# A pairwise bilinear kernel whose loads of fields and weights are asked for later in the text

## The chip, the cores and the metric

The kernel runs on one core of one Trainium2 chip. The metric is the device time of one execution in microseconds. Several executions are timed in rounds with executions of the kernel before on the same chip; ratios below are the mean time of one kernel's fast runs over that of the other's fast runs of the same rounds, so they are not quite the ratio of the medians.

## The reference

There are 32 fields of 128 numbers for 1024 rows, and for each of the 496 pairs i < j of fields a 128 x 128 weight. The output is 260 MB, so writing it is a large part of the work.

```python
I_IDX, J_IDX = pairs[:, 0], pairs[:, 1]          # all i < j of 32 fields, 496 pairs
v_i = inputs[:, I_IDX, :]                        # inputs: (1024, 32, 128) float32
v_j = inputs[:, J_IDX, :]
transformed = jnp.einsum('bpd,ped->bpe', v_i, W) # W: (496, 128, 128) float32
return transformed * v_j                         # (1024, 496, 128)
```

## The kernel before

The pairs are ordered by j, so that field j is first needed when j begins, after j(j-1)/2 pairs. Every field has a tile of its own and stays to the end. Weights come in chunks of eight pairs into four buffers. Two pairs share an output tile of 1 MB, and there are six such tiles.

```python
pairs = [(i, j) for j in range(1, 32) for i in range(j)]
xpool = tile_pool(name="x", bufs=1)      # tag=f"x{f}": a tile for each field
wpool = tile_pool(name="w", bufs=4)
opool = tile_pool(name="o", bufs=6)
ppool = tile_pool(name="ps", bufs=4, space=PSUM)
# ... load_x, load_w: dma_start of one field (512 KB) or one chunk (512 KB)
load_w(0, (0, 1, 3, WC))                 # on the ScalarE queue, three pieces
load_x(0, nc.sync, 2); load_x(1, nc.sync, 2); load_x(2, nc.sync)
load_w(1); load_x(3, nc.sync); load_w(2)
load_x(4, nc.scalar); load_x(5, nc.scalar)
for q, (i, j) in enumerate(pairs):
    if q % WC == 0 and q // WC + 3 < nchunk:
        load_w(q // WC + 3)              # three chunks ahead
    if i == 0 and 5 < j + 3 < NF:
        load_x(j + 3, nc.scalar)         # three fields ahead
    # two matmuls of 512 columns: po = w_q^T x_i
    # one VectorE product of 1024 columns: ot = po * x_j
    # after every second pair: dma_start of ot to the output, on the SyncE queue
```

Of the kernel before, what the change touches and what calls it, by code (L numbers as in the profile page):

```python
# [1 line left out]

# [4 lines left out]

F32 = mybir.dt.float32
ALU = mybir.AluOpType

P = 128
NF = 32
NQ = NF * (NF - 1) // 2
BT = 1024
HB = 512
WC = 8
OC = 2


def _pairs():  # L20

    return [(i, j) for j in range(1, NF) for i in range(j)]


@with_exitstack
def kernel(
    ctx: ExitStack,
    tc: tile.TileContext,
    xt: bass.AP,
    wt: bass.AP,  # L30
    out: bass.AP,
):






    nc = tc.nc
    pairs = _pairs()  # L40

    xpool = ctx.enter_context(tc.tile_pool(name="x", bufs=1))
    wpool = ctx.enter_context(tc.tile_pool(name="w", bufs=4))
    opool = ctx.enter_context(tc.tile_pool(name="o", bufs=6))
    ppool = ctx.enter_context(tc.tile_pool(name="ps", bufs=4, space=bass.MemoryType.PSUM))

    x_sb = {}

    def load_x(f, eng, pieces=1):
        x_sb[f] = xpool.tile([P, BT], F32, tag=f"x{f}", name=f"x_{f}")  # L50
        s = BT // pieces
        for k in range(pieces):
            eng.dma_start(out=x_sb[f][:, k * s : (k + 1) * s], in_=xt[:, f, k * s : (k + 1) * s])  # L53

    nchunk = NQ // WC
    w_sb = {}

    def load_w(c, splits=(0, WC)):
        w_sb[c] = wpool.tile([P, WC, P], F32, tag="w", name=f"w_{c}")
        for a, b in zip(splits, splits[1:]):  # L60
            nc.scalar.dma_start(out=w_sb[c][:, a:b, :], in_=wt[:, c * WC + a : c * WC + b, :])  # L61

    load_w(0, (0, 1, 3, WC))
    load_x(0, nc.sync, 2)
    load_x(1, nc.sync, 2)
    load_x(2, nc.sync)
    load_w(1)
    load_x(3, nc.sync)
    load_w(2)
    load_x(4, nc.scalar)  # L70
    load_x(5, nc.scalar)

    out_v = out.rearrange("q e b -> e q b")
    ot = None
    for q, (i, j) in enumerate(pairs):
        if q % WC == 0 and q // WC + 3 < nchunk:
            load_w(q // WC + 3)
        if i == 0 and 5 < j + 3 < NF:
            load_x(j + 3, nc.scalar)
        po = ppool.tile([P, BT], F32, tag="po", name=f"po_{q}")  # L80
        for h in range(0, BT, HB):
            nc.tensor.matmul(  # L82
                po[:, h : h + HB],
                w_sb[q // WC][:, q % WC, :],
                x_sb[i][:, h : h + HB],
                start=True,
                stop=True,
            )
        r = q % OC
        if r == 0:  # L90
            ot = opool.tile([P, OC, BT], F32, tag="ot", name=f"ot_{q}")
        if q < NQ - OC:
            nc.vector.tensor_tensor(ot[:, r, :], po[:, :], x_sb[j][:, :], ALU.mult)  # L93
            if r == OC - 1:
                nc.sync.dma_start(out=out_v[:, q - r : q + 1, :], in_=ot[:, :, :])  # L95
        else:
            for h in range(0, BT, HB):
                s = slice(h, h + HB)
                nc.vector.tensor_tensor(ot[:, r, s], po[:, s], x_sb[j][:, s], ALU.mult)  # L99
                nc.sync.dma_start(out=out_v[:, q, s], in_=ot[:, r, s])  # L100


# [25 lines left out]
```

## Time and profile before

| What | Before | How to read it |
|---|---|---|
| time, median of 3 | 877.84 us (877.59 to 878.51) | very steady, so 0.5% can be seen |
| span of the profiled run | 876.1 us | first to last instruction |
| PE busy | 856.6 us, 98% | TensorE is the bound over the whole |
| DVE busy | 606.3 us, 69% | the products lie beside the matmuls |
| DMA | 309.69 MB, mean 353 GB/s | 411 to 420 GB/s from 9 to 150 us, some 342 after |

In the views below PE stands for TensorE's matmuls, PEld for its weight loads, DVE for VectorE. A transfer is issued on the queue of an engine (ACTq for ScalarE, SPq for SyncE) and lands when the DMA engines have moved its bytes. A record is one entry of the trace; TensorE leaves four for each pair. The chain is the work that ended last, followed back to what released each step.

The means hide that there are two stages. After 150 us TensorE never stops. Before, the DMA engines are full, and TensorE is stopped at times.

### The profile page before, as it was taken

Reading aid. Unit: us, or ns where it says so; the run is one execution under the profiler, and the core shown is the slowest. Engines: PE = TensorE matmul, PEld = TensorE weight load, DVE = VectorE, ACT = ScalarE, POOL = GpSimd, SP = SyncE. Lnnn points to the kernel's source line nnn. Section 1 sums busy time; section 2 is a strip of 40 time slices with the busy share of each in tenths; the row PEclk is TensorE's granted clock in tenths of the full one; section 3 lists DMA queues with packets and bytes.
Section 4 is the critical chain, followed back from the end, with each engine's and each line's share of the span. In section 5 each row is a group of like instructions: output and inputs, shape, how many; then the busy total and the mean of one; then the engine's idle time right before and its main releaser. Section 6 shows DMA issues by size and latency. Waiting matters only on the chain.

```text
span 876.1 us, 5490 instructions
## 1 busy us (share of the span) xinstructions
PE 856.6 (98%) x1984; PEld 377.1 (43%) x1984; DVE 606.3 (69%) x498; POOL 0.2 (0%) x4
## 2 busy tenths in 40 slices
PE   8997899999999999999999999999999999999997
PEld 3432344444444444444444444444444444444443
DVE  4744677777777777777777777777777777777775
POOL 0000000000000000000000000000000000000000
PEclk9999999999999999999999999999999999999999
DMA  9999999989898898998988889888898989889877
GB/s 349 421 419 421 421 420 415 357 340 354 333 352 342 338 357 333 349 339 341 353 340 346 339 346 352 339 345 339 351 343 341 346 338 355 342 338 351 329 311 296
DMA packets 81898, 309.69 MB, mean 353 GB/s; under 512 B 5584, under 2 KB 5840, under 8 KB 81872
## 3 DMA queue, kind: packets, MB, share of 16 engines
q1 hardware_dynamic: 68624, 262.16, 75.3%
q10 hardware_dynamic: 13248, 47.19, 15.5%
q8 instruction: 15, 0.25, 0.1%
q14 instruction: 11, 0.09, 0.0%
HBM read 49.28 MB, written 260.05 MB: 353 GB/s over the span
## 4 chain that ended last, share of the span: by engine, by line
PE 88%; DMA 11%; DVE 0%; ACTq 0%; DVEq 0%; issue 0%; SPq 0%
PE po L82 88%; DMA x<-in_xt_dram 6%; DMA out_dram<-ot 3%; DMA w<-in_wt_dram 2%; DVE ot L93 0%; DVE ot L99 0%; DVEq L121 0%; ACTq L61 0%; ACTq L53 0%; DVEq L93 0%; SPq L95 0%
## 5 line engine op out<-in xcount | busy, mean ns | idle before, releaser
L82 PE MATMUL po<-x,w 128*128 128x512 f32 x1984 | 856.6, 594 | 13.9 <-DVE ot L93 9.9
L93 DVE TENSOR_TENSOR ot<-po,x 128x1024 f32<-128x1024 f32 x494 | 603.7, 1225 | 264.7 <-PE po L82 228.1
L82 PEld LDWEIGHTS po<-x,w 128*128 128x128 f32 x1984 | 377.1, 190 | 492.6 <-issue 470.0
L99 DVE TENSOR_TENSOR ot<-po,x 128x512 f32<-128x512 f32 x4 | 2.6, 687 | 0.9 <-PE po L82 0.9
L115 POOL MEMSET const-bfloat16-1.0<- 128x1 bf16 x1 | 0.1, 102 | 0.0
L115 POOL MEMSET const-uint8-127<- 128x1 uint8 x1 | 0.1, 102 | 0.0
L115 POOL MEMSET const-float32-0.0<- 128x1 f32 x1 | 0.1, 99 | 0.2 <-issue 0.2
L115 POOL MEMSET const-float32-1.0<- 128x1 f32 x1 | 0.1, 99 | 0.0
## 6 DMA issues: line engine op xcount, KB each, us to landing
out_dram<-ot SPq DMA_DIRECT2D x247, 1024.0 KB, 4.8
w<-in_wt_dram ACTq DMA_DIRECT2D x61, 512.0 KB, 4.3
x<-in_xt_dram ACTq DMA_DIRECT2D x28, 512.0 KB, 12.8
x<-in_xt_dram SPq DMA_DIRECT2D x4, 256.0 KB, 4.6
x<-in_xt_dram SPq DMA_DIRECT2D x2, 512.0 KB, 8.5
out_dram<-ot SPq DMA_DIRECT2D x4, 256.0 KB, 3.3
w<-in_wt_dram ACTq DMA_DIRECT2D x1, 320.0 KB, 6.3
w<-in_wt_dram ACTq DMA_DIRECT2D x1, 128.0 KB, 3.6
```

Source lines behind the costliest of these rows:

```text
L82: nc.tensor.matmul(po[:, h : h + HB], w_sb[q // WC][:, q % WC, :], x_sb[i][:, h : h + HB], start=True, stop=True,)
L93: nc.vector.tensor_tensor(ot[:, r, :], po[:, :], x_sb[j][:, :], ALU.mult)
L99: nc.vector.tensor_tensor(ot[:, r, s], po[:, s], x_sb[j][:, s], ALU.mult)
L115: nc = _bacc.Bacc("TRN2", target_bir_lowering=False, num_devices=1)
```

## The change

Its intent is to keep the early stage free of loads that are not yet needed: after a few early fields that keep a longer lead, a field is asked for one field ahead, and weights two chunks ahead instead of three. Nothing else differs.

```diff
     load_x(2, nc.sync)
-    load_w(1)
     load_x(3, nc.sync)
-    load_w(2)
-    load_x(4, nc.scalar)
-    load_x(5, nc.scalar)
+
+    def ahead(j):
+
+        return j + 3 if j <= 2 else j + 2 if j <= 5 else j + 1
...
     for q, (i, j) in enumerate(pairs):
-        if q % WC == 0 and q // WC + 3 < nchunk:
-            load_w(q // WC + 3)
-        if i == 0 and 5 < j + 3 < NF:
-            load_x(j + 3, nc.scalar)
+        if q % WC == 0 and q // WC + 2 < nchunk:
+            for c in (1, 2) if q == 0 else (q // WC + 2,):
+                load_w(c)
+        if i == 0:
+            for f in range(j + 1, min(ahead(j) + 1, NF)):
+                if f not in x_sb:
+                    load_x(f, nc.scalar)
```

## The prediction

> **What bounds the kernel now.** I read the page first, then the chain that ended last, the busy time in stretches, the waits of the SyncE queue, and the order of the issues on the ScalarE queue.
>
> ```profile
> span 876.1 us, 5490 instructions
> PE 856.6 (98%) x1984; PEld 377.1 (43%) x1984; DVE 606.3 (69%) x498; POOL 0.2 (0%) x4
> ...
> L82 PE MATMUL po<-x,w 128*128 128x512 f32 x1984 | 856.6, 594 | 13.9 <-DVE ot L93 9.9
> ...
> x<-in_xt_dram ACTq DMA_DIRECT2D x28, 512.0 KB, 12.8
> ```
>
> TensorE is the bound: there are 496 pairs, each with two matmuls of 512 columns, and the trace has 1984 records, so two per matmul and four per pair. The 594 ns are pipelined and overlap, so I take the pace from the chain instead:
>
> ```profile
> 42.11 14.41 DMA w<-in_wt_dram
> 56.54 12.74 DMA x<-in_xt_dram
> ...
> 69.31 15.24 DMA x<-in_xt_dram
> ...
> 97.73 772.78 PE po L82 x1800
> ```
>
> The last piece is 1800 records in 772.78 us, 0.4293 us each: 1.717 us per pair, and 1984 x 0.4293 = 851.7 us for the whole work. So only 876.1 - 851.7 = 24.4 us of the span are not matmuls at full pace. Before 97.7 us the chain is made of transfers, among them loads of weights and of fields: that is where the change can act. The same in stretches (columns: busy time of PE, PEld, DVE, POOL, then clock, DMA share, GB/s):
>
> ```profile
> 9.20:40.00 30.80, 30.80 (x73) 13.61 (x72) 22.49 (x19) 0.00 (x0) 1.00 1.02 411
> 40.00:97.70 57.70, 47.81 (x107) 19.29 (x105) 29.11 (x26) 0.00 (x0) 1.00 1.03 420
> 97.70:150.00 52.30, 52.27 (x122) 23.29 (x123) 39.04 (x33) 0.00 (x0) 1.00 1.02 418
> 150.00:870.50 720.50, 720.50 (x1679) 318.63 (x1677) 514.31 (x421) 0.00 (x0) 1.00 0.89 342
> ```
>
> From 9 to 150 us the DMA engines are full at 411 to 420 GB/s; afterwards 342 GB/s suffice and TensorE never stops. The loss is all in the second line: 107 records need 107 x 0.4293 = 45.9 us and the stretch has 57.7, so 11.8 us are lost. The remaining 12.6 us are the start (first matmul at 3.95 us, the first few at half pace, some 7 us together) and the tail of 5.6 us after 870.5; the change touches neither.
>
> Why are the DMA engines full early? The text of the kernel asks for field j+3 when field j begins, so field 31 is asked for at pair 28 x 27 / 2 = 378, which TensorE reaches at about 97.7 + (378 - 46) x 1.717 = 668 us. The trace has it otherwise. The issues on the ScalarE queue, in order (start, length of the run of issues, and how many):
>
> ```profile
> 0.73 3.35 ACTq L61 DMA_DIRECT2D w<-in_wt_dram  x5
> 4.64 3.63 ACTq L53 DMA_DIRECT2D x<-in_xt_dram  x2
> 10.06 0.34 ACTq L61 DMA_DIRECT2D w<-in_wt_dram  x1
> 10.44 12.57 ACTq L53 DMA_DIRECT2D x<-in_xt_dram  x5
> 23.11 0.43 ACTq L61 DMA_DIRECT2D w<-in_wt_dram  x1
> 23.57 18.44 ACTq L53 DMA_DIRECT2D x<-in_xt_dram  x8
> 42.11 0.44 ACTq L61 DMA_DIRECT2D w<-in_wt_dram  x1
> 46.68 16.10 ACTq L53 DMA_DIRECT2D x<-in_xt_dram  x8
> 64.22 0.33 ACTq L61 DMA_DIRECT2D w<-in_wt_dram  x1
> 67.22 12.52 ACTq L53 DMA_DIRECT2D x<-in_xt_dram  x5
> ```
>
> 2+5+8+8+5 = 28: all fields are issued by 79.7 us. They overtook the weight chunks that stand before them in the text. A fifth chunk has to wait for one of four buffers; a field has a tile of its own and waits for no buffer. So the build does not keep the order of the text on a queue: when the next load in the text has no buffer, it takes the next load that has one. And the outputs pay for it:
>
> ```profile
> SPq L95 <- DVE ot L93: 685.0, 234, 5.6
> SPq L95 <- DMA x<-in_xt_dram: 67.8, 17, 7.2
> ```
>
> The issue of an output waited 17 times, 67.8 us in all, for the landing of a field. The compiled program of the kernel before (the change was not built) says why: all transfers of both queues use eight completion semaphores in turn, and each waits until the transfer eight places earlier has landed.
>
> **What the Trainium skill says.** All from the page "DMA: Bandwidth & Descriptors". Section "Issuing engines are not separate DMA queues": transfers issued by different engines end up on the same 16 DMA engines and interleave. The trace agrees: loads on one queue and outputs on the other together make the 420 GB/s. Section "Specifications" gives a fabric ceiling of 435 GB/s and about 358 per core at the memory; the trace's plateau of 420 is near the first and above the second, so with this mix the second is not the limit. Section "Anatomy of one DMA — SWDGE (gpsimd) path": semaphore waits are made by the issuing sequencer, not by the DMA engines. The trace shows that for these queues too, in the 67.8 us on the SyncE queue.
>
> **The change, part by part.** It adds and removes no matmul, no product, no byte: 62 weight chunks and 32 fields, the same sizes and queues, four weight buffers and one tile for each field as before. It moves places in the text. I worked out the order on the ScalarE queue by the rule seen above (first in the text that has a buffer).
>
> Before, text order: w0 in three pieces, w1, w2, x4, x5; pair 0: w3; pair 3: x6; pair 6: x7; pair 8: w4; pair 10: x8; pair 15: x9. The rule gives w0 x3, w1, w2 (five), x4, x5 (two), w3 (one), x6 and following while w4 waits for chunk 0 to be finished: exactly the runs 5, 2, 1, 5 of the trace.
>
> After, text order: w0 in three pieces; pair 0: w1, w2, x4; pair 1: x5; pair 6: x6; pair 8: w3; pair 10: x7; pair 16: w4; pair 21: x8. The rule gives w0 x3, w1, w2, x4, x5, **x6, w3**, x7, x8 and so on while w4 waits for chunk 0.
>
> Weights: "two ahead" in the text means nothing while there are four buffers. Before, chunk c was asked for at the start of chunk c-3 and needed the buffer of c-4, just finished: issued at once. After, it is asked for one chunk later in the text, but its buffer is free at the same moment as before and nothing ahead of it in the queue waits longer, so it is pulled forward to the same moment. Cost 0.
>
> Fields: from x7 on, each has no buffer to wait for and comes as soon as the queue and its completion semaphore let it, in the same order as before. When w4, w5 and w6 get their buffers, the fields still outstanding (x11 and up, x19 and up, x27 and up) stand later in both texts, so the chunk goes first in both. Cost 0.
>
> The exchange of w3 and x6: both move 512 KB, so each takes the other's place and semaphore. x6 starts at about 10.06 instead of 10.44 us, w3 0.4 us later than before. w3 is needed at pair 24, some 46 us; x6 at pair 15, about 34 us; landings in this stretch take at most 16.5 us. Cost 0. The SyncE queue has x0 to x3 and then the outputs in the same order.
>
> Sum: 877.84 + 0 = 877.8 us. The full DMA engines and the 11.8 us of stall stay.
>
> **Rivals.** (1) The order of the text is kept, as the change seems to intend. By pair 46, the end of the stall, only fields up to about x11 would be loaded instead of x31: 20 x 0.524 MB = 10.5 MB less, at 420 GB/s 25 us of DMA time, more than the 11.8 us of stall. The gain would be at most those: 877.8 - 11.8 = 866.0 us, 1.3% faster and still within 2%. For it speaks the bottleneck in the 40 to 97.7 us stretch; against it the kernel before, whose text also spreads its fields to pair 378 and whose trace has them all by 80 us. I give it 6%.
>
> (2) A wait for a late load. If loads really were issued late, x8 would be asked for 7 pairs, 7 x 1.717 = 12.0 us, before its first use, and the median landing of a field is 12.8 us: about 1 us of waiting there, less for later fields whose lead grows by 1.7 us each. Chunks would have two chunks of 13.7 us each, 27.5 us, against at most 15.2 us. Together +1 to +3 us, 880 us, and only if rival 1's order holds, whose gain is larger. 2%.
>
> (3) The queues interleave otherwise: a small shift on one queue puts a field and an output into exchanged places among the eight semaphores. One field is 0.524 MB / 420 GB/s = 1.25 us, so the stall grows or shrinks by one or two such steps: 875.3 to 880.3 us. Some 8%.
>
> **Range and chances.** The three runs of before lie within 0.9 us; with rival 3 and some difference between runs I put the range at 875.0 to 880.3 us, most of it close to 877.8. Faster by over 2% needs 17.6 us, more than the whole stall of 11.8: 1%. Slower by over 2% would need many loads to arrive late: 1%. Within 2%: 98%.
>
> **What would show it right or wrong.** Right: the runs on the ScalarE queue read 5, then three fields (x4, x5, x6), then one chunk, then four fields, then as before; all 28 fields issued by about 80 us; the SyncE queue still waits some 68 us for fields; about 107 PE records and 420 GB/s between 40 and 97.7 us; the last piece of the chain about 1800 records. Wrong at the step "the build reorders": fields issued past 200 us, under 400 GB/s before 100 us, no wait of outputs for fields, a time near 866. Wrong at "weights come at the same moment": waits of matmuls for weights after 10 us.

## The result, and the profile after

| | Before | After |
|---|---|---|
| median of 4 runs | 878.17 us (877.59 to 878.66) | 877.85 us (877.67 to 878.52) |
| ratio, 95% interval | | 0.9998 (0.9981 to 1.0015) |
| span, granted clock | 876.1 us, 0.998 | 876.0 us, 0.999 |

The two kernels take the same time. First, the issues on the ScalarE queue of the changed kernel (start, length of the run, number), to be laid beside the runs 5, 2, 1, 5, 1, 8, 1, 8, 1, 5 of before:

```profile
0.72 3.42 ACTq L61 DMA_DIRECT2D w<-in_wt_dram  x5
4.69 6.13 ACTq L53 DMA_DIRECT2D x<-in_xt_dram  x3
10.86 0.45 ACTq L61 DMA_DIRECT2D w<-in_wt_dram  x1
12.18 11.59 ACTq L53 DMA_DIRECT2D x<-in_xt_dram  x4
23.87 0.47 ACTq L61 DMA_DIRECT2D w<-in_wt_dram  x1
24.38 18.90 ACTq L53 DMA_DIRECT2D x<-in_xt_dram  x8
43.38 0.46 ACTq L61 DMA_DIRECT2D w<-in_wt_dram  x1
47.71 15.42 ACTq L53 DMA_DIRECT2D x<-in_xt_dram  x8
64.90 0.33 ACTq L61 DMA_DIRECT2D w<-in_wt_dram  x1
67.04 13.00 ACTq L53 DMA_DIRECT2D x<-in_xt_dram  x5
```

One field has changed places with one chunk: 3, 1, 4 in place of 2, 1, 5. All 28 fields of this queue are issued by 80.0 us, as before by 79.7, though the text asks for the last of them later than ever. The compiled programs of the two kernels, compared transfer by transfer over all 349, differ in this exchange alone.

The same stretches of the changed kernel as shown for before (busy PE, PEld, DVE, POOL, then clock, DMA share, GB/s):

```profile
9.20:40.00 30.80, 30.80 (x73) 13.62 (x72) 22.81 (x19) 0.00 (x0) 1.00 1.02 413
40.00:97.70 57.70, 47.40 (x107) 19.10 (x105) 28.59 (x26) 0.00 (x0) 1.00 1.03 420
97.70:150.00 52.30, 52.30 (x122) 23.28 (x123) 39.13 (x33) 0.00 (x0) 1.00 1.02 418
```

There are the same 107 matmul records in the second stretch, and the same 420 GB/s. The waits of the SyncE queue (total us, times, longest) and the last long piece of the chain:

```profile
SPq L98 <- DMA x<-in_xt_dram: 65.8, 15, 7.2
```

```profile
97.70 772.78 PE po L85 x1800
```

The outputs still wait for fields, 65.8 us against 67.8, and the last 1800 records begin at 97.70 us, as they did at 97.73.

### The profile page after: what moved, and what is told of

Its sections match the earlier page's. It is cut to its first block, busy times and chain, and to the rows that moved or that the text cites. A ratio compares the mean times of both kernels' runs of the same rounds, so it can differ in the third digit from the quotient of the medians.

```text
span 876.0 us, 5490 instructions
## 1 busy us (share of the span) xinstructions
PE 856.1 (98%) x1984; PEld 376.9 (43%) x1984; DVE 605.1 (69%) x498; POOL 0.2 (0%) x4
## 4 chain that ended last, share of the span: by engine, by line
PE 88%; DMA 11%; DVE 0%; ACTq 0%; DVEq 0%; issue 0%; SPq 0%
PE po L85 88%; DMA x<-in_xt_dram 6%; DMA out_dram<-ot 3%; DMA w<-in_wt_dram 2%; DVE ot L96 0%; DVE ot L102 0%; DVEq L124 0%; ACTq L61 0%; ACTq L53 0%; DVEq L96 0%; SPq L98 0%
## 6 DMA issues: line engine op xcount, KB each, us to landing
x<-in_xt_dram ACTq DMA_DIRECT2D x28, 512.0 KB, 12.8
```

## The experiments

The theory: the place of a load in the text does not decide when it is issued, because the build pulls forward on its queue the loads that have a buffer; the early fields fill the DMA engines, and their bytes are what stops TensorE. The means to test it is a call that pins an instruction behind the one traced before it on its engine (`tc.keep_in_program_order`). By the compiled program it adds order, no transfer: there are 349 with it and without.

### The changed kernel with the order of the text held

```diff
-            eng.dma_start(out=x_sb[f][...], in_=xt[...])
+            tc.keep_in_program_order(eng.dma_start(out=x_sb[f][...], in_=xt[...]))
...
-            nc.scalar.dma_start(out=w_sb[c][...], in_=wt[...])
+            tc.keep_in_program_order(nc.scalar.dma_start(out=w_sb[c][...], in_=wt[...]))
```

The edit to `load_x` also pins the four fields of the SyncE queue, which stand before all outputs with and without it.

> The changed kernel, with every load on the ScalarE queue pinned behind the load before it in the text, so that the order of the text holds. Theory (the build pulls all fields to the front, their bytes fill the DMA engines and cost the 11.8 us of stall between 40 and 97.7 us): fields are spread to the end, the stall goes, 866.0 us (864.5 to 868.5), no waits of outputs for fields worth over 5 us, DMA at 340 to 390 GB/s after 40 us, between 40 and 97.7 us some 134 PE records instead of 107. Rival 1 (the stall has another cause, such as the outputs themselves or the start): 876 to 879 us. Rival 2 (one field ahead is too late once the order holds): waits of PE or DVE for fields after 30 us, 868 to 880 us.

Measured: 865.76 us (865.63 to 865.84), ratio to before 0.9862 (0.9847 to 0.9876), correct. The ScalarE queue, the stretch and the chain of this kernel:

```profile
12.21 0.33 ACTq L53 DMA_DIRECT2D x<-in_xt_dram  x1
20.51 0.33 ACTq L61 DMA_DIRECT2D w<-in_wt_dram  x1
22.95 0.34 ACTq L53 DMA_DIRECT2D x<-in_xt_dram  x1
34.24 0.34 ACTq L61 DMA_DIRECT2D w<-in_wt_dram  x1
34.62 0.78 ACTq L53 DMA_DIRECT2D x<-in_xt_dram  x1
```

```profile
40.00:97.70 57.70, 57.70 (x136) 25.60 (x135) 41.01 (x34) 0.00 (x0) 1.00 1.01 399
```

```profile
0.73 3.26 DMA w<-in_wt_dram
...
4.03 854.19 PE po L85 x1984
```

One field now goes with one chunk, and the chunks come 13.7 us apart, which is TensorE's own pace for eight pairs. The stretch has 136 records instead of 107, and the chain is one piece of TensorE from 4 us to the end. The DMA rate in the stretch was 399 GB/s, above the 390 that I had expected as its upper end; it no longer stops anything. Outputs waited for a field once, 2.4 us. So the stall goes when the fields come in the order of the text; the change alone did not bring that about. The Trainium skill, "Perfetto Trace Analysis", section "Optimization Strategy", says that where the most contended engine changes over time it can pay to interleave the regimes; this run agrees: the field loads moved out of the full stage cost nothing in the later one.

### The kernel before with its order held

The same two lines, in the kernel before.

> The kernel before, pinned in the same way: three fields and three chunks ahead. Theory: what counts is that the order holds, not the lead; by 97.7 us it has loaded two fields (2.5 us of DMA time) more than the changed kernel pinned, but there is slack of over 10 us, so again 866.0 us, within 1 us of the other pinned kernel. Rival (the lead is what counts, and the change is worth something when it takes effect): 868 to 872 us, with 2 us or more of stall left before 98 us.

Measured: 865.35 us (864.97 to 866.05), ratio 0.9856 (0.9839 to 0.9872), with no wait of VectorE for an output. Between this and the pinned changed kernel there is no difference that the intervals can tell. The chain of this kernel is one piece too:

```profile
4.04 854.67 PE po L82 x1984
```

The shorter lead of the change is worth nothing here either; holding the order brings the whole gain. With four buffers the lead takes effect only in part (by 97.7 us the pinned kernel before has issued 11 fields on this queue, the pinned changed one 9); with three, further below, it is close to that of the text.

### Part of the fields pinned: what does one early field cost?

Only the fields above a limit are pinned; the others are pulled forward as before. Weights are not pinned.

```diff
-            eng.dma_start(out=x_sb[f][...], in_=xt[...])
+            d = eng.dma_start(out=x_sb[f][...], in_=xt[...])
+            if f > 18:                  # and in two more kernels 24, 21
+                tc.keep_in_program_order(d)
```

> The changed kernel with only fields 19 to 31 pinned; fields up to 18 are still pulled forward. Theory (bytes: 25 us of early DMA time too many, of which 13 us were absorbed by buffers and 11.8 us became stall): leaving out 13 fields takes 13 x 1.25 = 16 us of early DMA time away, more than the stall, so 866 to 867.5 us. Rival (each wait of an output for a field costs its share: the stall is proportional to the number of fields pulled forward, 12 of 25 remain): half of the stall remains, about 872 us.

> The changed kernel with only fields 25 to 31 pinned; fields up to 24 are pulled forward. Theory (bytes, each field 1.25 us of DMA time, all of it stall once the buffers are full): 7 x 1.25 = 8.7 us less than 877.8, so 869.1 us (868 to 870.5). Rival (proportional to the number of fields pulled forward, 18 of 25 remain): 877.8 - 12 x 7 / 25 = 874.4 us.

> The changed kernel with only fields 22 to 31 pinned. Theory, mended after the run with fields 25 to 31 pinned: in the full stretch 8 fields go with 8 pairs of output and one weight chunk, 8 x 0.524 + 0.524 + 8 x 0.524 = 8.9 MB, 21.2 us at 420 GB/s, where TensorE needs 13.7 us: 7.5 us of stall for 8 fields, 0.93 us for each, not 1.25, because the spare rate of the DMA engines takes the rest. Ten fields fewer: 878.2 - 9.3 = 868.9 us (868.2 to 869.8). First form of the theory (1.25 us each): 865.7 us. Rival (proportional to the number pulled forward, 12.6 us x 15 / 25 remain): 873.1 us.

The limits were run in the order 18, 24, 21; the last expectation was written after the second had missed.

| Fields pinned | Time, us (lowest to highest) | Ratio to before | Expected | PE records, 40 to 97.7 us |
|---|---|---|---|---|
| none (the change) | 877.85 (877.67 to 878.52) | 0.9998 | | 107 |
| 25 to 31 | 871.72 (871.58 to 871.92) | 0.9924 | 869.1, missed | 123 |
| 22 to 31 | 868.87 (868.67 to 870.22) | 0.9898 | 868.9, mended theory | 128 |
| 19 to 31 | 866.79 (866.2 to 867.3) | 0.9873 | 866 to 867.5 | 131 |
| all | 865.76 (865.63 to 865.84) | 0.9862 | 866.0 | 136 |

The first result fitted, but it could not tell the cost of one field: at 1.25 or at 0.93 us, thirteen fields are worth more than the 11.8 us of stall. The second fell between theory (869.1) and rival (874.4): seven fields were worth 878.72 - 871.72 = 7.0 us against before in the same rounds, 1.0 us each and not 1.25. My step was wrong that a field's whole DMA time becomes stall. In the full stretch eight fields go with eight pairs of output and one chunk, 8.9 MB, 21.2 us at 420 GB/s, where TensorE alone takes 13.7: 7.5 us for eight fields, 0.93 us each. The rest is taken by the spare rate of the DMA engines (420 GB/s against the some 343 that the work needs later). The trace agrees with the 21.2 us: in the changed kernel the chunks were issued at 43.38 and 64.90 us with eight fields between them, 21.5 us apart. The mended theory then gave 868.9 for ten fields, and 868.87 was measured, well off both other forms (865.7 and 873.1). Such a hit to 0.1 us is partly luck: the four runs spread from 868.67 to 870.22. Thirteen fields take nearly the whole stall away. The fifteen that are then still early, fields 4 to 18, were all issued by 42 us in the kernel before as well, where TensorE first stopped at 58.2 us; that these are absorbed while the output tiles fill is my reading, not shown by a run.

### Turns without bytes

A completion semaphore is the counter that tells that a transfer has landed. The compiled program gives every transfer one of eight in turn. Is it the turns that cost, or the bytes? The pinned changed kernel got 22 free loads of 8 bytes a partition into tiles that nobody reads.

```diff
+    def dummy(f):
+        t = tiny.tile([P, 2], F32, tag=f"t{f}", name=f"t_{f}")
+        nc.scalar.dma_start(out=t[:, :], in_=xt[:, f, 0:2])
...
+        if i == 0 and 7 <= j <= 28:
+            dummy(j + 3)
```

> The pinned changed kernel with 22 extra loads of 8 bytes a partition, into tiles that nobody reads, left free so that they are pulled forward among the first outputs as the fields were: they take turns of the eight completion semaphores, but move no bytes to speak of. Theory (bytes make the stall): 865.8 us (865 to 867), no waits of DVE for outputs over 2 us. Rival (the turns make it: each output waits for a load eight places earlier, whatever its size): waits of outputs for loads of tens of us and 870 to 878 us.

Measured: 865.18 us (865.0 to 865.81), ratio 0.985 (0.9836 to 0.9865). All 22 were pulled forward, and outputs did wait for them:

```profile
14.41 12.42 ACTq L62 DMA_DIRECT2D t<-in_xt_dram  x9
...
28.60 11.99 ACTq L62 DMA_DIRECT2D t<-in_xt_dram  x13
```

```profile
SPq L106 <- DMA out_dram<-ot: 15.3, 6, 8.3
SPq L106 <- DMA t<-in_xt_dram: 9.3, 4, 7.1
```

The outputs were held up, 9.3 us for the small loads and 15.3 us for other outputs, yet nothing of it reached TensorE. So these turns delay outputs but did not stop the kernel, which points to the bytes. A limit of this test: the small loads were done by 41 us, earlier than the fields of the changed kernel, so it does not exclude that turns cost something while the DMA engines are full. The stretch from 40 to 97.7 us of the changed kernel narrows that down: with a DMA share of 1.03 and 420 GB/s, the highest of its stretches, the turns left no DMA time unused. What they do fix is the order in which the bytes pass: in the compiled program an output stands after every two or three fields, and none can overtake. Whether the same early fields with another order would stop TensorE less was not tried.

### Three weight buffers

```diff
-    wpool = ctx.enter_context(tc.tile_pool(name="w", bufs=4))
+    wpool = ctx.enter_context(tc.tile_pool(name="w", bufs=3))
```

> The changed kernel with three weight buffers instead of four: now a chunk really comes two chunks ahead. Theory: two chunks are 27.5 us against landings of at most 16.5 us, so no wait for weights after 10 us; the fields are still all pulled forward, the same bytes are in the first 98 us: 877.8 us (876 to 880). Rival (weights two ahead are too late while the DMA engines are full): waits of PE for weights, 880 to 890 us.

> The pinned changed kernel with three weight buffers: the leads are now really those of the text, two chunks, and a field asked for right behind a chunk. Theory (leads of 27 us for chunks and 24 us or more for fields are above the landing times of some 5 to 16 us): the same time as pinned with four buffers, 865.8 us (865 to 867), no wait for a load after the start. Rival (too short a lead with full DMA engines): waits for weights or fields after 10 us, 868 us or more.

Measured: in the changed kernel 877.0 us (876.58 to 877.47), ratio 0.999 (0.9975 to 1.0005); with the order held as well 865.4 us (864.74 to 865.69), ratio 0.9853 (0.9836 to 0.9869). The ScalarE queue of the first:

```profile
4.65 18.04 ACTq L53 DMA_DIRECT2D x<-in_xt_dram  x8
22.79 0.41 ACTq L61 DMA_DIRECT2D w<-in_wt_dram  x1
```

The fourth chunk, which came after three fields at 10.86 us in the changed kernel, now comes after eight, at 22.79 us: it waits for a buffer. So the number of buffers sets the lead of the weights, and the "+ 2" or "+ 3" in the text does not. Neither kernel waits for a chunk after the start; with the order held, chunks land in 3.7 to 6.3 us after the first 30 us. In the pinned one a weight load of TensorE waited once more for a field, 0.7 us, at 9.9 us, so still in the start; the matmuls ran on without a stop.

### Two more output tiles

The kernel with three weight buffers got two more output tiles; these take 2 MB, more than the 512 KB of the weight buffer that was given up.

```diff
-    wpool = ctx.enter_context(tc.tile_pool(name="w", bufs=4))
-    opool = ctx.enter_context(tc.tile_pool(name="o", bufs=6))
+    wpool = ctx.enter_context(tc.tile_pool(name="w", bufs=3))
+    opool = ctx.enter_context(tc.tile_pool(name="o", bufs=8))
```

> The changed kernel (nothing pinned) with three weight buffers and eight output tiles instead of six. Theory (TensorE stops when the output tiles are full): two tiles more let it run 4 pairs further ahead of the outputs, 4 x 1.717 = 6.9 us less stall than the 877.0 us of three weight buffers with six tiles: 870.1 us (869 to 871.5), with the DMA engines just as full. Rival (the stall follows the bytes alone and tiles only move it in time): 876 to 878 us.

Measured: 872.47 us (871.42 to 873.74), ratio 0.9935 (0.992 to 0.995): 4.5 us less than with six tiles, where I expected 6.9, and outside my range. The profiled run is the slowest of the four (873.74; the others 871.42, 871.69 and 873.25, without a trace), so what follows explains that run and may be more than the other runs lost. Three views of it, the timeline of TensorE, the ScalarE queue, and the stretches around the gap (PE busy, PEld, DVE, POOL, clock, DMA share, GB/s):

```profile
37.69 38.36 PE L85 MATMUL po<-x,w 128*128 128x512 f32 x89
80.04 20.48 PE L85 MATMUL po<-x,w 128*128 128x512 f32 x41 [3.99 <-DMA w<-in_wt_dram]
```

```profile
46.88 16.50 ACTq L53 DMA_DIRECT2D x<-in_xt_dram  x8
65.18 0.33 ACTq L61 DMA_DIRECT2D w<-in_wt_dram  x1
```

```profile
80.00:82.00 2.00, 1.96 (x3) 0.96 (x4) 0.00 (x0) 0.00 (x0) 0.50 1.02 416
82.00:84.00 2.00, 2.00 (x4) 0.90 (x3) 0.17 (x1) 0.00 (x0) 0.50 1.03 424
...
86.00:88.00 2.00, 2.00 (x6) 0.85 (x5) 1.23 (x1) 0.00 (x0) 1.00 1.02 420
```

TensorE no longer stopped for outputs in this stretch; a wait for a weight chunk took the place. That chunk was issued at 65.18 us and took 14.7 us to land. Its buffer should have been free since pair 24, some 48 us; it stood in the queue behind eight fields issued from 46.88 us on, each of which waits, in the compiled program, for the landing of the transfer eight places earlier. So the lead of two chunks, 27.5 us by the buffers, had shrunk to some 11 us by the place in the queue. After the 4.0 us gap the granted clock was 0.50 until about 85.3 us: the weight loads from 80.0 to 85.3 us came 0.86 us apart instead of 0.43, so about six records lost another 2.6 us. The Trainium skill, "TensorE: Matmul & The Clock Gate", section "What's actually happening", says that an idle window of some 3.4 us brings the array down to half its clock. This run agrees on the half, 0.50 after 4.0 us of gap, but not on the time: the clock had fallen by some 78.5 us, about 2.5 us after the last matmul ended by the profile, which models these ends. How much two output tiles alone would save stays open, since the weight wait gave the outputs time to catch up.

## Why the prediction was right

**TensorE is the bound, and the loss is 11.8 us in one stretch.** Right. With the order held TensorE ran 1984 records in 854.19 us without a stop, and the time fell by 878.01 - 865.76 = 12.2 us in the same rounds.

**The build pulls loads forward by buffer, not by text.** Right, and the step that carried everything. The forecast order came out in each run of issues (5, 3, 1, 4, and so on). The equal times alone would say little, since a change that is worth nothing for any other reason gives them too; the issues, and the 12.2 us that holding the order brings, say more. What the rule does not give is the number of eight fields between two chunks: the prediction took it over from the trace, and why it is eight stays open.

**Weights: same moment, cost 0.** Right; three buffers moved the fourth chunk by 12 us, the text only by the exchange below.

**The exchange of a field and a chunk: cost 0.** Right in cost. I put the chunk 0.4 us later; it was 0.8 (10.86 against 10.06 us), which nothing waited for.

**The rivals.** The gain of the first, 866.0 us, was the right size for a kernel whose order holds (865.76). The second, a wait for late loads, was too gloomy: in the pinned changed kernel each field lands in 5.5 to 8.9 us after the first 30 us, against a median of 12.8 us before, and the buffers still bring loads earlier than the text. The third, another interleaving of the queues, did not happen: all eight runs of the two kernels lie between 877.59 and 878.66 us.

**What was off in the working.** In the third rival, and in the expectation for seven pinned fields, I reckoned a field's full DMA time, 1.25 us, as stall. It costs 0.93 us by the mended sum, and 1.0 us was measured over seven fields. The total did not depend on it, since the stall was read from the profile and not built up from fields.

## What to carry to other kernels

Before moving a load in the text, look at the order of issues in the trace: if loads stand far before the point where the text asks for them, buffers and the build set their time, and the move may do nothing, as here. To delay a load, tie it to something that comes late: here a place in the queue behind a load that waits for a buffer did it for the fields, and fewer buffers for the weights. Loads that are "free" because nobody waits for them are not free while outputs fill the DMA engines: here holding the order gained 1.4% with no other edit.

## What the Trainium skill lacked or had wrong

- "DMA: Bandwidth & Descriptors", section "Issuing engines are not separate DMA queues": it has the shared DMA engines, but no page says that queues can also hold each other up before issue, by completion semaphores that a build shares among them. In the changed kernel outputs on the SyncE queue waited 65.8 us in 15 waits for fields, nearly all of them issued on the ScalarE queue.
- The same page, section "Where 436 GB/s comes from": it says that for traffic between HBM and SBUF the HBM side, about 358 GB/s, binds, and in the same paragraph calls 425 GB/s, measured on one core's loads, near the rate of the fabric. For one core alone the first does not hold: with loads and outputs mixed it had 420 GB/s from 40 to 97.7 us.
- No page says that the order of the text on a queue is not the order of issue: field 31, asked for at about 668 us by the text of the kernel before (an estimate from TensorE's pace), was issued by 79.7 us.
